# An edge-message kernel: rows gathered by GpSimd alone, where SyncE brought seven groups row by row

## The chip, the core and the metric

The kernel runs on one core of a Trainium2 chip. The metric is the device time in microseconds of one execution. A profile was taken of one execution, and all engine names below are those of the profile: PE is the matrix engine TensorE (PEld its weight loads), DVE is VectorE, ACT is ScalarE, POOL is GpSimd, SP is SyncE, which here only issues DMAs and loads registers.

## What is computed

One layer of a graph network on 12,500 nodes with 128 features and 400,000 edges, sorted by their target `dst`; `src` is random. Each edge has 32 attributes. Cut to what matters:

```
h   = relu(layernorm(x))
m   = relu(concat(h[src], h[dst], ea) @ w1 + b1) @ w2 + b2
agg = segment_sum(m, dst)
gi  = agg @ w_ih + b_ih ;  gh = h @ w_hh + b_hh
r, z = sigmoid of the first two thirds of gi + gh
n   = tanh(third of gi + r * third of gh)
out = x + (1 - z) * n + z * h
```

All is float32. `w1` has three blocks of rows: for `h[src]`, for `h[dst]` and for the attributes.

## The kernel before

**Prelude.** The nodes are normalised, transposed into `hT_all` (kept on chip), and multiplied by the first block of `w1`; the product `A = h @ w1a`, 12,500 rows of 512 bytes, is written to DRAM. In this way an edge's part from its source node is one row of `A`.

**Edge loop.** Edges go in tiles of 128; eight tiles are a double group (391 of them, the first with five tiles), and a double group is done as two units of four tiles (782 units `u`, `k, h = divmod(u, 2)`). For a double group the kernel needs eight tiles of rows of `A`, one for each edge: buffer `G`, 128 partitions by 8 by 128 floats. Then, for each unit:

- `pre` (L576): TensorE adds the target node's part and the attributes' part, from `L` (a one-hot matrix of targets in its upper half, made by VectorE at L479 out of `Ld`, and the attributes in its lower half) and `RW` (rows of the target nodes' window and of `w1`);
- `add` (L595): VectorE adds the PSUM result to `G`, in place;
- `relu` (L601): ScalarE writes the relu to `RB`. With the relu of the second unit the buffer `G` comes free;
- `seg` (L614): TensorE sums the rows by target with one-hot weights `OH`; `take` (L622, L623) copies the sums of a double group out of PSUM.

After every 14 double groups a generator `node` does the gates for a block of 512 nodes, one step a unit.

**How rows come.** `gather(k)` (L125) issues eight indirect DMAs on POOL, one for each tile of 128 rows, with the row numbers in `src_i`. `G` is a pool of `GBUFS` = 8 buffers, and `gathers(u)` asks for a double group when the taker of its buffer (`taker`, `ring`) is near its end in program order; at run time the gather waits for the relu that frees the buffer. The first `RAW` = 8 double groups are gathered before `A` is there: they fetch rows of `x` instead, and `raw_stats`, `raw_fin`, `raw_h`, `raw_turn` normalise, transpose and multiply them within the loop.

Seven double groups (`by_hand`: 70, 122, 174, 225, 277, 329, 381) are not gathered by POOL. For each, SyncE issues 1024 DMAs of one row of 512 bytes into a buffer of their own, `G_sp` (L753). `job_indices` loads the row numbers (L739), one VectorE instruction multiplies them by 512 (L849), SyncE loads 32 of them at a time into registers (L747), and each DMA takes its source address from a register. `run_jobs(u, phase)` spreads the issues evenly over the units between two such groups, four times a unit.

**Orders.** The schedule is written by hand (`manual_schedule`): each engine does its instructions in program order. SyncE's queue holds, besides the row DMAs, the loads that the loop lives on: `fetch_d` (L472, two broadcast loads of `Ld` for two double groups), `fetch` (L463, the load of `L`'s attributes for two double groups), the index tiles `src_i` and `dst_i`, and the node blocks' `xb` and `out`. POOL's queue holds the gathers alone, once the loop runs. `L` and `Ld` have three buffers each; `L` for double groups `k + 4` and `k + 5` is asked for at `k`.

Of the kernel before, what the change touches and what calls it, by code (L numbers as in the profile page):

```python
# [8 lines left out]
F32 = mybir.dt.float32  # L9
F16 = mybir.dt.float16  # L10
I32 = mybir.dt.int32
U8 = mybir.dt.uint8
BF16 = mybir.dt.bfloat16
ET = mybir.EngineType
AF = mybir.ActivationFunctionType
ALU = mybir.AluOpType
AX = mybir.AxisListType

N, E, D, DE = 12500, 400000, 128, 32
T = E // 128  # L20

GRP = 4
PAIR = 2 * GRP
SUP0 = T % PAIR
NP = T // PAIR + 1
# [11 lines left out]
NT = -(-N // 128)  # L37
NFULL = N // 128
BAT = (4,) + (8,) * 11 + (NFULL - 92, 1)
RAW = 8  # L40
GBUFS = 8
PLACE = 20
CH = PLACE * PAIR
LOAD = 32
STEP = 2
SP_PAIRS = 7
NR = 12672

ROW = 512


@with_exitstack
def tile_gnn(ctx: ExitStack, tc: tile.TileContext, x, src, srcT, dstT, dstP, eaT, eaP, w1, b1, w2T, b2,
             wih, bih, whh, bhh, out):
    nc = tc.nc
    ctx.enter_context(tc.manual_schedule())
    const = ctx.enter_context(tc.tile_pool(name="const", bufs=1))
    hT_all = const.tile([128, N], F32, name="hT_all")
    gp = ctx.enter_context(tc.tile_pool(name="gp", bufs=GBUFS))
    p2 = ctx.enter_context(tc.tile_pool(name="p2", bufs=2))  # L60
# [5 lines left out]
    def tiles(k):  # L66
        return (0 if k == 0 else SUP0 + (k - 1) * PAIR, SUP0 + k * PAIR)


    def unit_tiles(u):  # L70
        k, h = divmod(u, 2)
        t0, t1 = tiles(k)
        return [(t0 + a * GRP + j, j, a) for j in (2 * h, 2 * h + 1) for a in range(2)
                if t0 + a * GRP + j < t1]

    JOBS0 = 14

    by_hand = [JOBS0 + 5 + int((i + 1) * (NP - 15 - JOBS0) / SP_PAIRS) for i in range(SP_PAIRS)]


    src_i = {}
# [23 lines left out]
    A = dram.tile([N, D], F32, name="A")  # L105
# [2 lines left out]

    G = {}

    taker, ring = {}, []
    for k in range(NP):
        if k not in by_hand:
            taker[k] = ring[-GBUFS] if len(ring) >= GBUFS else -1
            ring.append(k)

    def gather(k):
        if k >= NP or k in by_hand:
            return
        G[k] = gp.tile([128, GRP, 2, D], F32, name="G")  # L120
        table = x if k < RAW else A
        for u in (2 * k, 2 * k + 1):
            for t, j, a in unit_tiles(u):
                c, i = divmod(t, CH)
                nc.gpsimd.indirect_dma_start(  # L125
                    out=G[k][:, j, a, :], out_offset=None, in_=table,
                    in_offset=bass.IndirectOffsetOnAxis(ap=src_i[c][:, i:i + 1], axis=0))

    for k in range(RAW):
        gather(k)  # L130
# [58 lines left out]
    with tc.tile_pool(name="pp", bufs=3) as pp:  # L189
# [50 lines left out]
        rows = const.tile([1, 6 * D + D], F32, name="rows")  # L240
# [18 lines left out]
        def chunk(q):  # L259
            b, c = chunks[q]  # L260
            i0, n = bats[b]
            return b, i0, c, min(n, c + 4), PB(b), (i0 + c) * 128
# [3 lines left out]
        for q in range(NC + 3):  # L266
            if q < NC:
                b, i0, c, e, P, n0 = chunk(q)
# [3 lines left out]
            if 1 <= q <= NC:  # L272
                b, i0, c, e, P, n0 = chunk(q - 1)
# [6 lines left out]
            if q >= 3:  # L280
                b, i0, c, e, P, n0 = chunk(q - 3)
# [4 lines left out]
            if q < NC:  # L286
                b, i0, c, e, P, n0 = chunk(q)
# [4 lines left out]
            if 1 <= q <= NC:  # L292
                b, i0, c, e, P, n0 = chunk(q - 1)
# [3 lines left out]
            if q >= 3:  # L297
                b, i0, c, e, P, n0 = chunk(q - 3)
                if e == bats[b][1]:
                    nc.sync.dma_start(nodes(A, i0, e, P), asb[b][:P, :e, :])  # L300
            if 2 <= q <= NC + 1:
                b, i0, c, e, P, n0 = chunk(q - 2)
# [4 lines left out]
        for b0, b1, n in ((0, 1, BAT[0]), (1, 12, 8), (12, 13, BAT[12])):  # L307
            i0 = sum(BAT[:b0])
            for b in range(b0, b1):
                i = i0 + (b - b0) * n  # L310
# [32 lines left out]
    for a in range(2):  # L343
        s = slice(V * a, V * (a + 1))
        nc.vector.tensor_scalar(node_of[s, :], base_b[s, :, a], place_c[s, :], float(-V * a),
                                op0=ALU.add, op1=ALU.add)
# [110 lines left out]
    def fetch(q):  # L457
        if q * QP >= NP:
            return
        n = min(QP, NP - q * QP)  # L460
        Ls[q] = p3.tile([128, QP * 512], F32, name="L")
        c = slice(q * QP * 512, (q * QP + n) * 512)
        nc.sync.dma_start(Ls[q][2 * V:, :n * 512], eaP[:, c])  # L463
# [72 lines left out]
    def slots(u):  # L536
        return [(j % 2) * 2 + a for _, j, a in unit_tiles(u)]

    def raw_h(u):
        if u < 2 * RAW:  # L540
            for i, s in enumerate(slots(u)):
                relu_norm(unit(u)[:, s, :], unit(u)[:, s, :], HE[u][:, i, :])

    def raw_stats(u):
        if u < 2 * RAW:
            l = slots(u)
            HE[u] = bn_sqrt(p2, bn(p2, lambda j: unit(u)[:, l[j], :], 128, len(l)), 128, len(l))

    def raw_fin(u):
        if u < 2 * RAW:  # L550
            n = len(slots(u))
            st = p2.tile([128, GRP, 2], F32, name="st_raw", bufs=4)
            bn_fin(p2, st[:, :n, :], HE[u], 128, n)
            HE[u] = st

    def raw_turn(u):
        if u < 2 * RAW:
            l = slots(u)
            pt = ps1.tile([128, 512], F32, name="misc")
            for i, s in enumerate(l):  # L560
                nc.tensor.transpose(pt[:, i * 128:(i + 1) * 128], unit(u)[:, s, :], ident)
            hT = p3.tile([128, 512], F32, name="hTe", bufs=2)
            nc.vector.tensor_copy(hT[:, :len(l) * 128], pt[:, :len(l) * 128])
            HE[u] = hT
# [163 lines left out]
        return o  # L728


    late = ExitStack()
    pj = late.enter_context(tc.tile_pool(name="pj", bufs=1, side="right"))
    NJ = len(by_hand)
    A_bytes = A.bitcast(U8).rearrange("n f -> (n f)")
    at = const.tile([NJ, PAIR * 128], I32, name="at")

    def job_indices(r):
        t0 = tiles(by_hand[r])[0]
        nc.sync.dma_start(at[r:r + 1, :], src[t0 * 128:(t0 + PAIR) * 128].rearrange(  # L739
            "(o e) -> o e", o=1))  # L740

    def one_by_one(r):
        k = by_hand[r]
        G[k] = pj.tile([128, GRP, 2, D], F32, name="G_sp")
        rows = G[k].bitcast(U8)
        for e0 in range(0, PAIR * 128, LOAD):
            _, vals = nc.values_load_multi_w_load_instructions(  # L747
                at[r:r + 1, e0:e0 + LOAD], engines=[ET.SP], min_val=0, max_val=ROW * (N - 1),
                skip_runtime_bounds_check_because="src holds numbers of nodes")
            for i, v in enumerate(vals):  # L750
                e = e0 + i
                a, j = divmod(e // 128, GRP)
                nc.sync.dma_start(rows[e % 128:e % 128 + 1, j, a, :],  # L753
                                  A_bytes[bass.ds(v, ROW)].rearrange("(o f) -> o f", o=1))
                if i % STEP == STEP - 1:
                    yield


    PH = 4
    live = []  # L760

    def run_jobs(u, phase):
        if phase == 0:
            for r, k in enumerate(by_hand):
                begin = 2 * by_hand[r - 1] + 2 if r else 2 * JOBS0
                if u == begin:
                    live[:] = [one_by_one(r), u, 2 * k - 8 - begin, 0]
        if live:
            it, begin, span, _ = live
            want = -(-(PAIR * 128 // STEP) * ((u - begin) * PH + phase + 1) // (span * PH))  # L770
            while live and live[3] < want:
                live[3] += 1
                if next(it, "end") == "end":
                    live.clear()


    asked = [RAW]

    def gathers(u):
        while asked[0] < NP and (asked[0] in by_hand or 2 * taker[asked[0]] + 1 < u + 2):  # L780
            gather(asked[0])
            asked[0] += 1

# [46 lines left out]
    for u in range(NU):  # L830
        k, h = divmod(u, 2)
        gathers(u)
        if h == 0:
            if k % QP == 0:
                fetch_d(k // QP + 3)
                fetch(k // QP + 2)
            if k % BP == 0 and k:
                nodes_left.append([node(k // BP - 1), 0])
            if k % PLACE == 1:
                indices(k // PLACE + 2)  # L840
            if k % PLACE == 5:
                place(k // PLACE + 1)
                dst_tile(k // PLACE + 2)
            if k == NP - 20:
                check_windows()
        for r in range(u, min(u + 1, NJ)):
            job_indices(r)
        if u == 2 * JOBS0 - 2:
            nc.vector.tensor_scalar(at, at, float(ROW), None, op0=ALU.mult)  # L849

        def other(phase):
            run_jobs(u, phase)
            if h == 0 and phase == 1:
                window(k + 3)
            if h == 0 and phase == 3:
                window_rows(k + 3)
            if phase == 3:
                step(nodes_left)

        other(0)  # L860
        if h == 0:
            take(k - 1)
        stages(u)
        other(1)
        other(2)
        seg(u)
        if u == 0:
            node_setup()
        other(3)
# [4 lines left out]

    late.close()
    fb = ctx.enter_context(tc.tile_pool(name="fb", bufs=1, side="right"))

    def general_setup():  # L880
# [94 lines left out]
    f = nc.values_load(flag[0:1, 0:1], min_val=0, max_val=1)  # L975
# [67 lines left out]
```

## Time and profile before

| what | value |
|---|---|
| time, median of 3 runs | 5573.1 us (5562.81, 5573.1, 5592.95) |
| profiled execution, its own time | 5562.81 us |
| span of the profiled execution | 5561.0 us |
| granted TensorE clock, mean | 0.674 |
| busy: PE, PEld | 2693.6 us (48%), 1588.2 us (29%) |
| busy: DVE, ACT, POOL | 1494.3 us (27%), 678.7 us (12%), 2932.6 us (53%) |
| indirect gathers of `A` on POOL (L125) | 3008, mean 955 ns |
| row DMAs on SP (L753) | 7168 of 0.5 KB |
| DMA engines' time taken by POOL's queue, SP's queue | 14.5%, 8.9% |

The busy shares are means over the whole span; no engine is near 100%. In the lists of waits, a line gives who waited, for whom, the time in total, the number of times and the longest; "remote" is a wait that the profile can't put down to an instruction. In a timeline, a line gives the start and the length in us, engine, source line, operation and tiles, how many instructions are merged, and in brackets the idle time ahead of them with what ended it. SP's instructions are only issues: the length is that of issuing, not of the transfer.

### The profile page before, as it was taken

What the parts mean: (1) busy time and instruction counts of PE and PEld (TensorE: products, weight loads), DVE (VectorE), ACT (ScalarE), POOL (GpSimd) and SP (SyncE); (2) the same over time, 40 slices, a digit from 0 to 9 for tenths busy, and PEclk for the clock granted to TensorE, in tenths of its full rate; (3) what the DMA queues carried; (4) which work ended last, traced back from release to release, by engine and by line L of the source; (5) the groups of instructions that cost most, each with busy time, mean ns of one, the idle gap of its engine ahead of it and who ended that gap; (6) DMA issues with size and microseconds to landing.
All of it is one profiled execution on the core that took longest, in us unless ns stands there. A gap on an engine that the chain in (4) does not pass through costs nothing. (4 is left out here: it accounts for less than half of the span.)

```text
span 5561.0 us, 57483 instructions
## 1 busy us (share of the span) xinstructions
PE 2693.6 (48%) x12938; PEld 1588.2 (29%) x12938; DVE 1494.3 (27%) x4097; ACT 678.7 (12%) x1460; POOL 2932.6 (53%) x3077
## 2 busy tenths in 40 slices
PE   4554554455445544444444454444455445544446
PEld 3432222232222322222222232222222222322223
DVE  5522222222222222222222222222222222222223
ACT  3211111111011111111111111100111111111111
POOL 4455555555455555455555546555455554655452
PEclk8766666676666666666666676666676666666667
DMA  3322222222122222222222222222222222222121
GB/s 118 72 62 58 65 60 58 74 57 63 51 63 54 68 58 57 55 63 67 57 55 61 60 66 57 58 59 58 71 58 57 61 55 56 68 62 59 51 63 52
DMA packets 168791, 342.80 MB, mean 62 GB/s; under 512 B 70653, under 2 KB 83752, under 8 KB 168447
## 3 DMA queue, kind: packets, MB, share of 16 engines
q0 software_dynamic: 98208, 201.33, 14.5%
q1 hardware_dynamic: 70095, 137.71, 8.9%
q8 instruction: 107, 1.75, 0.1%
q14 instruction: 237, 1.94, 0.1%
q10 hardware_dynamic: 144, 0.07, 0.0%
HBM read 324.99 MB, written 13.84 MB: 61 GB/s over the span
## 5 line engine op out<-in xcount | busy, mean ns | idle before, releaser
L125 POOL DMA_INDIRECT G<-A,src_i x3008 | 2873.8, 955 | 2550.7 <-ACT RB L601 1269.7
L576 PE MATMUL pre<-RW,L 128*128 128x256 f32 x3128 | 1231.4, 530 | 1820.1 <-DMA L<-in_eaP 1467.5
L576 PEld LDWEIGHTS pre<-RW,L 128*128 128x128 f32 x3128 | 740.6, 260 | 2178.7 <-issue 2025.8
L622 DVE COPY sums<-seg 64x128 f32<-64x128 f32 x391 | 110.1, 282 | 2602.9 <-PE seg L614 1183.5
L601 ACT ACTIVATE RB<-G 128x512 f32<-128x512 f32 x752 | 474.3, 631 | 1746.3 <-DVE G L595 844.7
L614 PE MATMUL seg<-RB,OH 128*32 128x129 f32 x6250 | 642.4, 340 | 3.5 <-issue 3.5
L501 PE MATMUL oh<-w1b,hw 128*64 128x128 f32 x782 | 204.4, 351 | 749.8 <-DVE hw L498 537.7
L595 DVE TENSOR_TENSOR G<-pre,G 128x512 f32<-128x512 f32 x752 | 514.1, 684 | 11.2 <-PE pre L576 0.3
L510 DVE TENSOR_TENSOR RW<-oh,b1b 32x128 f32<-32x128 f32 x782 | 219.6, 281 | 802.1 <-remote 284.1
L614 PEld LDWEIGHTS seg<-RB,OH 128*32 128x32 f32 x6250 | 348.9, 130 | 259.8 <-issue 167.7
L623 ACT CAST dcol<-seg 64x1 f16<-64x1 f32 x391 | 60.5, 155 | 2805.5 <-DVE sums L622 1873.3
L501 PEld LDWEIGHTS oh<-w1b,hw 128*64 128x64 f32 x782 | 88.4, 160 | 930.0 <-DVE hw L498 650.5
L479 DVE TENSOR_SCALAR L<-Ld,node_of 64x512 f32<-64x512 int32 x391 | 187.0, 478 | 0.2 <-issue 0.2
L528 DVE TENSOR_TENSOR OH<-dloc,iota 128x256 f32<-128x256 f16 (+1 forms) x392 | 165.9, 423 | 7.9 <-issue 0.6
L645 PE MATMUL nd<-spot,sums 64*128 64x40 f32 x782 | 131.4, 341 | 17.2 <-issue 17.2
L645 PEld LDWEIGHTS nd<-spot,sums 64*128 64x128 f32 x782 | 128.0, 254 | 30.6 <-issue 30.6
L630 DVE TENSOR_TENSOR TOT<-nd,TOT 128x192 f32<-128x192 f32 x28 | 10.0, 358 | 411.2 <-remote 344.2
L650 PE MATMUL misc<-spot_h,dcol 128*128 128x40 f16 x391 | 37.5, 200 | 153.2 <-issue 153.2
L609 PE MATMUL seg<-zrow 1*64 1x129 bf16 x391 | 102.7, 263 | 0.0
L498 DVE COPY hw<-hT_all 128x64 f32 x391 | 86.0, 220 | 17.4 <-DVE G L595 9.3
L305 PE MATMUL pre<-w1a,hT_all 128*128 128x128 f32 x196 | 51.6, 412 | 60.2 <-remote 30.2
L664 PE MATMUL misc<-DEG,brow 33*128 33x512 f32 x112 | 77.5, 778 | 0.1
(143 smaller groups left out, 1242.2 us busy)
## 6 DMA issues: line engine op xcount, KB each, us to landing
G_sp<-A SPq DMA_DIRECT2D x7168, 0.5 KB
Ld<-in_dstP SPq DMA_DIRECT2D x390, 128.0 KB
L<-in_eaP SPq DMA_DIRECT2D x195, 256.0 KB
G<-A,src_i POOLq DMA_INDIRECT x3008
xb<-in_x SPq DMA_DIRECT2D x28, 256.0 KB
out<-xb SPq DMA_DIRECT2D x28, 256.0 KB
xs<-in_x SPq DMA_DIRECT2D x11, 512.0 KB
A<-asb SPq DMA_DIRECT2D x11, 512.0 KB
```

Of the source, the lines that this page charges most:

```text
L125: nc.gpsimd.indirect_dma_start(out=G[k][:, j, a, :], out_offset=None, in_=table, in_offset=bass.IndirectOffsetOnAxis(ap=src_i[c][:, i:i + ...
L479: nc.vector.tensor_scalar(Ls[k // QP][:2 * V, c], Ds[k // QP][:, c], node_of[:, k:k + 1], None, op0=ALU.is_equal)
L501: nc.tensor.matmul(PB_[k][:2 * V, :D], hw.rearrange("p a v -> p (a v)"), w1b, start=True, stop=True)
L510: nc.vector.tensor_tensor(RW[k % 4][s, a, :], pm[s, :D], b1b[s, :], op=ALU.add)
L528: nc.vector.tensor_tensor(o, d.to_broadcast(shape), i.to_broadcast(shape), op=ALU.is_equal)
L576: nc.tensor.matmul(PP[u][:, 2 * i:2 * i + 2, :], Ls[k // QP][:, c0:c0 + 128], RW[k % 4], start=True, stop=not raw)
L595: nc.vector.tensor_tensor(RT[u], PP.pop(u), RT[u], op=ALU.add)
L601: nc.scalar.activation(o[:, :, :D], RT.pop(u), AF.Relu)
L609: nc.tensor.matmul(SEG[k][:2 * V, :D + 1], zrow[:, :2 * V], zrow[:, :D + 1], start=True, stop=False)
L614: nc.tensor.matmul(SEG[k][V * a:V * (a + 1), :D + 1], OH[k][:, j, a, :], RB[u % 3][:, (j % 2) * 2 + a, :D + 1], start=False, stop=all(b != ...
L622: nc.vector.tensor_copy(sums[:, k % BP, :], pm[:2 * V, :D])
L645: nc.tensor.matmul(pt[:, bass.ds(offs[i], V + SHIFT)], sums[:, i, :], spot, start=False, stop=i == n - 1)
```

## The change

The seven double groups are gathered by POOL like all others. `by_hand`, `taker`, `ring`, the pool `pj` with `G_sp`, the table `at`, `job_indices`, `one_by_one` and `run_jobs` are taken out with all that they issue. `RAW` and `GBUFS` become 9: the pool `G` has nine buffers, and nine double groups take rows of `x`. `gathers(u)` asks for double group `k` when group `k - 9` is near its end. The loop's other steps and their order stay.

```
-RAW = 8
-GBUFS = 8
+RAW = 9
+GBUFS = 9
-LOAD = 32
-STEP = 2
-SP_PAIRS = 7
-ROW = 512
...
-    JOBS0 = 14
-    by_hand = [JOBS0 + 5 + int((i + 1) * (NP - 15 - JOBS0) / SP_PAIRS) for i in range(SP_PAIRS)]
...
-    taker, ring = {}, []
-    for k in range(NP):
-        if k not in by_hand:
-            taker[k] = ring[-GBUFS] if len(ring) >= GBUFS else -1
-            ring.append(k)
     def gather(k):
-        if k >= NP or k in by_hand:
+        if k >= NP:
             return
...
-    def one_by_one(r):
-        k = by_hand[r]
-        G[k] = pj.tile([128, GRP, 2, D], F32, name="G_sp")
-        rows = G[k].bitcast(U8)
-        for e0 in range(0, PAIR * 128, LOAD):
-            _, vals = nc.values_load_multi_w_load_instructions(
-                at[r:r + 1, e0:e0 + LOAD], engines=[ET.SP], min_val=0, max_val=ROW * (N - 1),
-                skip_runtime_bounds_check_because="src holds numbers of nodes")
-            for i, v in enumerate(vals):
-                e = e0 + i
-                a, j = divmod(e // 128, GRP)
-                nc.sync.dma_start(rows[e % 128:e % 128 + 1, j, a, :],
-                                  A_bytes[bass.ds(v, ROW)].rearrange("(o f) -> o f", o=1))
-                if i % STEP == STEP - 1:
-                    yield
...
     def gathers(u):
-        while asked[0] < NP and (asked[0] in by_hand or 2 * taker[asked[0]] + 1 < u + 2):
+        while asked[0] < NP and 2 * (asked[0] - GBUFS) + 1 < u + 2:
             gather(asked[0])
             asked[0] += 1
...
-        for r in range(u, min(u + 1, NJ)):
-            job_indices(r)
-        if u == 2 * JOBS0 - 2:
-            nc.vector.tensor_scalar(at, at, float(ROW), None, op0=ALU.mult)
...
-            run_jobs(u, phase)
```

More of the change, by code (lines that the diff above doesn't have):

```diff
@@ L728, in gates @@
         return o
[L731 to L740, printed above, removed]
-    def one_by_one(r):
-        k = by_hand[r]
-        G[k] = pj.tile([128, GRP, 2, D], F32, name="G_sp")
-        rows = G[k].bitcast(U8)
-        for e0 in range(0, PAIR * 128, LOAD):
-            _, vals = nc.values_load_multi_w_load_instructions(
-                at[r:r + 1, e0:e0 + LOAD], engines=[ET.SP], min_val=0, max_val=ROW * (N - 1),
-                skip_runtime_bounds_check_because="src holds numbers of nodes")
-            for i, v in enumerate(vals):
-                e = e0 + i
-                a, j = divmod(e // 128, GRP)
-                nc.sync.dma_start(rows[e % 128:e % 128 + 1, j, a, :],
-                                  A_bytes[bass.ds(v, ROW)].rearrange("(o f) -> o f", o=1))
-                if i % STEP == STEP - 1:
-                    yield
[L759 to L774, printed above, removed]
     asked = [RAW]
     def gathers(u):
-        while asked[0] < NP and (asked[0] in by_hand or 2 * taker[asked[0]] + 1 < u + 2):
+        while asked[0] < NP and 2 * (asked[0] - GBUFS) + 1 < u + 2:
             gather(asked[0])
@@ L873, in tile_gnn @@
         run(it)
-    late.close()
     fb = ctx.enter_context(tc.tile_pool(name="fb", bufs=1, side="right"))
```

## The prediction

> **What bounds the kernel now.** I read the summary of waits first, then SyncE's own timeline, then POOL's, and went back to the prelude for what they left unexplained.
>
> ```profile
> PE pre L576 <- DMA L<-in_eaP: 1467.5, 118, 24.8
> POOL G L125 <- ACT RB L601: 1269.7, 153, 22.4
> ```
>
> Columns: who waited, for whom, us in total, times, longest. TensorE waits for `L`, the edge attributes, and POOL waits for a row buffer that ScalarE's relu must free. TensorE is 48% busy, POOL 53%: neither is full. Why is `L` late? SyncE's timeline over one period, and TensorE's at the same place:
>
> ```profile
> 826.76 23.03 SPq L753 DMA_DIRECT2D G_sp<-A  x36
> 849.89 0.79 SPq L472 DMA_DIRECT2D Ld<-in_dstP  x2
> 850.95 0.30 SPq L463 DMA_DIRECT2D L<-in_eaP  x1
> ```
>
> ```profile
> 854.85 2.04 PE L576 MATMUL pre<-RW,L 128*128 128x256 f32 x4 [9.52 <-DMA L<-in_eaP]
> ```
>
> 36 row transfers (L753) stand ahead of two `Ld` loads and one `L` load in SyncE's order; `L` is issued at 850.95, and 3.9 us later its first matmul starts, after 9.52 us of idle TensorE. The rows never let up: jobs of 1024 rows run from 343.2 to 1099.8, 1121.1 to 1843.7, and so on to 5472.8, 0.69 to 0.74 us a row. So SyncE is full from 343 to 5473 us, and the pace of the edge loop is its pace. Where `L` was issued 10 us or less before its matmul (129 pairs of groups after group 40), a double group takes 14.58 us by the relus.
>
> **But a second limit lies close behind.** One gather (L125) takes 0.95 us and the next starts 1.25 us after it, so eight make 10.0 us a double group; POOL does this in runs. Two places without any row transfer, group starts 279 to 341 and the prelude:
>
> ```profile
> 279.09 0.94 POOL L125 DMA_INDIRECT G<-A,src_i  x1 [5.21 <-ACT RB L601]
> ...
> 302.58 0.95 POOL L125 DMA_INDIRECT G<-A,src_i  x1 [3.50 <-ACT dcol L623]
> ...
> 341.47 0.94 POOL L125 DMA_INDIRECT G<-A,src_i  x1 [8.84 <-ACT RB L601]
> ```
>
> ```profile
> 313.07 0.69 DVE L595 TENSOR_TENSOR G<-pre,G 128x512 f32<-128x512 f32 x1
> 336.51 0.28 DVE L622 COPY sums<-seg 64x128 f32<-64x128 f32 x1 [22.75 <-remote]
> ```
>
> ```profile
> 57.96 0.18 DVE L162 BATCH_NORM_AGGREGATE mv<-bn 128x2 f32<-128x6 f32 x1 [1.22 <-DVE mv L162]
> 59.36 0.18 DVE L162 BATCH_NORM_AGGREGATE mv<-bn 128x2 f32<-128x6 f32 x1 [1.22 <-DVE mv L162]
> ...
> 88.76 0.51 DVE L162 BATCH_NORM_AGGREGATE mv<-bn 128x2 f32<-128x6 f32 x6 [1.21 <-DVE mv L162]
> ```
>
> POOL gathers without a pause from 302.58 to 332.6. In that run VectorE stands still from 313.8 to 336.5, waiting for matmuls that the trace has started at 312.7; 3.9 us after the run ends, it goes on. In the prelude POOL gathers from 3.2 to 79.4, and six aggregates that take 0.51 us together after it come 1.40 us apart within it. The rows tell the same: sorted by how long POOL had been gathering without a pause, the median from one row's issue to the next is 0.32 us in the first 2 us, about 0.7 from 4 to 12, 1.4 from 12 to 16, 2.1 from 16 to 20, and 0.32 again 2 us after the run. A long run of gathers makes everybody else's signals late; what carries them I can't see. POOL then runs out of free buffers, pauses, and the others catch up.
>
> **The change part by part.**
>
> *Row transfers, registers, tables taken out (L747, L753, L739, L849).* 7168 issues, 224 register loads, seven loads and one 0.67 us VectorE instruction go. What counts is the order of SyncE's queue: `Ld` and `L` loads then wait for buffers alone. Without rows, before 343 us, `L` was issued 35 to 68 us ahead of its first matmul, so the 1467.5 us wait goes. What is late next is not a load but POOL's buffer, by the cycle above.
>
> *Seven groups go to POOL.* 56 gathers, of which 8 are the new raw ones: 48 more of `A`, 48 x 1.25 = 60 us of POOL. Each waits for a relu that frees its buffer; behind it on POOL stand only later gathers, and the additions of its own group wait for it. In the sum they are groups at the loop's price like the others, and 1.25 us for 128 rows stands against 128 x 0.70 = 90 us on SyncE. The Trainium skill (Perfetto Trace Analysis, section DMA Optimizations) advises the opposite: where descriptor generation is the limit, spread DMAs over sync, scalar and GPSIMD. By that rule alone POOL's 60 us would be added and the time would be 5623 us; this trace shows SyncE, not POOL, without slack.
>
> *RAW 8 to 9.* Eight more gathers of `x` at the start: 10 us on POOL between 79.4 and 173.5, where it idles 93.94 us; without that cover they would cost those 10 us. The two additional raw units cost statistics, 8 transposes and 8 matmuls in the turnover of the raw groups, which runs at (279.09 - 173.50) / 8 = 13.2 us a group; I charge the ninth at that.
>
> *One pool of nine.* Eight plus the single `G_sp` were nine before, so it is the same memory. A deeper ring lets POOL run further ahead; where POOL waits for the relu, that moves when the wait falls, not how long. I put it at 0. Its ends: a run of three groups instead of two at the longest pause of 8.84 us is (30 + 8.84) / 3 = 12.9 us a group, at the shortest of 3.5 us 11.2; a run that starves the others more is rival 1.
>
> *Pace of the loop without rows.* No long stretch shows it, so I bound it. Row-free and released by a relu at both ends: group 16 starts on POOL at 279.09, group 21 at 341.47, 62.4 / 5 = 12.48 us a group. By relus of units 16 and 28: (344.26 - 275.50) / 6 = 11.46. With rows, but `L` not late, seven stretches of 6 to 26 groups: 11.66, 12.36, 12.59, 12.63, 12.95, 14.0, 14.46, mean 12.98; the part of the first that has rows (344.3 to 612.2) gives 13.4. From below: the shortest pause (3.5 us) after the longest run (30 us, three groups) gives 11.2. I take 12.48, the row-free one, as it has POOL's runs and pauses in it. It holds no node block, which is against it, and no SyncE competing, as after the change.
>
> **The sum**, on the profiled execution: it took 5562.81 us, 1.8 of it outside its span of 5561.0. It is the lowest of the three runs; their median, 5573.1, is 0.2% above it.
> - to the first gather of `A`: 173.5
> - nine groups at 13.2: 118.8
> - groups 18 to 390, 373 at 12.48: 4655.0
> - from POOL's last gather (5504.0) to the end (5561.0): 57.0, kept, because then as now about eight gathered groups and a node block follow
> - outside the span: 1.8
>
> Together 5006 us, 10% less. Fixed are 351.1 us, so each 0.1 us a group is 37 us, and the kernel before is met at (5562.8 - 351.1) / 373 = 13.97 us a group.
>
> **Rivals.**
> 1. *Slower: starvation takes the place of the late load.* Each wait for `L` now forces POOL to pause (it gathers 71% of the time from 350 to 5450) and the queue of signals to drain. Without it runs grow, and a group costs what the longest row-free pause says: a run of two groups and 8.84 us, 14.4 us a group; 351 + 373 x 14.4 = 5722 us. For it: two of the seven stretches, 14.0 and 14.46; VectorE's 22.75 us wait after 11 us of a run; the added node work. Against it: five stretches below 13, and 14.58 where `L` is late. It decides from 13.97 us a group.
> 2. *POOL becomes the bound.* If the starving came mostly from the rows, POOL would never pause: 351 + 373 x 10.0 = 4081 us. For it: TensorE's work, at 6.9 us a group (2693.6 / 391), and VectorE's, 3.8, fit into 10. Against it: both row-free places starve.
> 3. *The change doesn't free the loads.* SyncE's issues are themselves slow while POOL runs; if `L` stayed late for that alone, only POOL's 60 us would be felt, within some 1% of before. Against it: 35 to 68 us of lead before 343 us.
>
> **How the numbers follow.** About 0.5% is what can be told from no change. The forecast's case has 0.80: from 11.2 us a group (4529) to 13.7, midway between 13.4 and the first slow stretch, 14.0 (5461). Rival 1 has 0.12, rival 3 0.03, rival 2 0.05. The range 4510 to 5460 is the first case with its bounds. Faster by over 0.5%: 0.80 + 0.05 = 0.85; within: 0.03; slower: 0.12.
>
> **What would show it.** In the changed profile no L753; TensorE's wait for `L` near zero; `L` issued tens of us ahead; POOL's share at 10.0 / 12.48 = 80% of the loop counting its gaps, in runs of 16 to 24 gathers and pauses of 3 to 9 us released by the relu; VectorE's long waits for `seg` inside those runs. The step on the row-free pace is wrong if POOL runs without pauses, or if runs get longer than 24 and pauses longer than 9 us; the step on SyncE is wrong if TensorE still waits for `L`.

## The result, and the profile after

| | before | after |
|---|---|---|
| median of 4 runs each | 5575.1 us (5562.81 to 5592.95) | 5023.4 us (5009.07 to 5032.93) |
| ratio, 95% interval | | 0.9006 [0.8973, 0.9039] |
| profiled execution, its span | 5562.81, 5561.0 | 5009.07, 5006.8 |
| granted TensorE clock | 0.674 | 0.693 |

The forecast was 5006. The profile of the changed kernel, first its busy shares and the group of gathers (busy time, mean ns of one, idle time ahead of them):

```profile
PE 2635.2 (53%) x12962; PEld 1565.6 (31%) x12962; DVE 1499.5 (30%) x4124; ACT 678.2 (14%) x1470; POOL 2973.4 (59%) x3133
...
L111 POOL DMA_INDIRECT G<-A,src_i x3056 | 2907.2, 951 | 1945.1 <-issue 875.7
```

48 more gathers than before, and POOL idles 606 us less ahead of them (2550.7 in the kernel before). In the summary of waits no line has TensorE waiting for `L`; the wait for POOL's buffer has halved, from 1269.7 us, and the longest is VectorE's for the sums (who waits, for whom, us, times, longest):

```profile
DVE sums L608 <- remote: 1520.4, 139, 26.3
...
POOL G L111 <- ACT RB L587: 621.2, 125, 12.2
```

SyncE's timeline, two periods of loads:

```profile
1004.72 0.78 SPq L458 DMA_DIRECT2D Ld<-in_dstP  x2
1008.26 0.48 SPq L449 DMA_DIRECT2D L<-in_eaP  x1
1021.97 0.78 SPq L458 DMA_DIRECT2D Ld<-in_dstP  x2
1022.84 0.54 SPq L449 DMA_DIRECT2D L<-in_eaP  x1
```

Between these loads SyncE has little to do; its own longest wait is for a buffer of `Ld`, which VectorE must have read:

```profile
SPq L458 <- DVE L L465: 2198.0, 100, 36.5
```

`L` is issued 36 to 66 us ahead of its first matmul for nine pairs of groups in ten, and never less than 17.7, where the median before was 4.0. POOL's timeline, only the gathers that end a pause:

```profile
1014.99 0.94 POOL L111 DMA_INDIRECT G<-A,src_i  x1 [3.23 <-ACT dcol L609]
...
1038.68 0.94 POOL L111 DMA_INDIRECT G<-A,src_i  x1 [4.04 <-ACT dcol L609]
...
1062.11 0.94 POOL L111 DMA_INDIRECT G<-A,src_i  x1 [3.72 <-ACT RB L587]
```

So POOL gathers from 1014.99 to 1034.6 without a pause (1038.68 - 4.04). VectorE in that run:

```profile
1026.12 0.69 DVE L581 TENSOR_TENSOR G<-pre,G 128x512 f32<-128x512 f32 x1
1037.89 0.28 DVE L608 COPY sums<-seg 64x128 f32<-64x128 f32 x1 [11.08 <-remote]
```

It stands still for 11 us, 7.8 of them while POOL gathers, and goes on 3.3 us after the run has ended, as in the kernel before. Over the loop (groups 18 to 390, a pause being an idle time of over 0.5 us) the runs are of 8 (63 times), 16 (100), 24 (33) and 32 gathers (2). The 199 pauses are 4.8 us in the mean, against 7.4 before; 48 are under 3 us, 21 over 9, the longest 10.05.

### The profile page after: what moved, and what is told of

The parts are those of the page before. It is cut to its first block, busy times and chain, and to the rows that moved or that the text cites. A ratio compares the mean times of both kernels' runs of the same rounds, so it can differ in the third digit from the quotient of the medians.

```text
span 5006.8 us, 43030 instructions
## 1 busy us (share of the span) xinstructions
PE 2635.2 (53%) x12962; PEld 1565.6 (31%) x12962; DVE 1499.5 (30%) x4124; ACT 678.2 (14%) x1470; POOL 2973.4 (59%) x3133
## 4 chain that ended last, share of the span: by engine, by line
PE 36%; another core or an unknown queue 32%; issue 15%; DVE 12%; POOL 2%; ACTq 1%; DMA 1%; DVEq 1%; ACT 0%; SPq 0%; POOLq 0%
PE pre L562 13%; PE seg L600 9%; DVE G L581 4%; PE oh L487 3%; POOL G L111 2%; PE nd L631 2%; PE nd L650 1%; PE nd L654 1%; PE seg L595 1%; DVE OH L514 1%; ACTq L587 1%; DVE RW L496 1%; PE misc L650 1%; PE misc L652 1%
## 5 line engine op out<-in xcount | busy, mean ns | idle before, releaser
L111 POOL DMA_INDIRECT G<-A,src_i x3056 | 2907.2, 951 | 1945.1 <-issue 875.7
L562 PE MATMUL pre<-RW,L 128*128 128x256 f32 x3128 | 1148.3, 500 | 304.0 <-DVE G L581 148.3
L487 PE MATMUL oh<-w1b,hw 128*64 128x128 f32 x782 | 215.1, 367 | 1751.4 <-DVE hw L484 1271.6
L562 PEld LDWEIGHTS pre<-RW,L 128*128 128x128 f32 x3128 | 694.2, 243 | 629.1 <-issue 525.3
L608 DVE COPY sums<-seg 64x128 f32<-64x128 f32 x391 | 110.1, 281 | 2048.3 <-remote 1520.4
L631 PE MATMUL nd<-spot,sums 64*128 64x40 f32 x782 | 146.3, 347 | 115.0 <-issue 114.8
L631 PEld LDWEIGHTS nd<-spot,sums 64*128 64x128 f32 x782 | 145.0, 272 | 120.7 <-issue 120.7
L650 PE MATMUL nd<-DEG,brow 33*128 33x512 f32 x112 | 81.6, 816 | 1.0 <-DVE DEG L618 1.0
L654 PE MATMUL nd<-TOT,w2ih 128*128 128x512 f32 x112 | 79.0, 796 | 0.0
```

Source lines behind the costliest of these rows:

```text
L111: nc.gpsimd.indirect_dma_start(out=G[k][:, j, a, :], out_offset=None, in_=table, in_offset=bass.IndirectOffsetOnAxis(ap=src_i[c][:, i:i + ...
L487: nc.tensor.matmul(PB_[k][:2 * V, :D], hw.rearrange("p a v -> p (a v)"), w1b, start=True, stop=True)
L562: nc.tensor.matmul(PP[u][:, 2 * i:2 * i + 2, :], Ls[k // QP][:, c0:c0 + 128], RW[k % 4], start=True, stop=not raw)
L631: nc.tensor.matmul(pt[:, bass.ds(offs[i], V + SHIFT)], sums[:, i, :], spot, start=False, stop=i == n - 1)
L650: nc.tensor.matmul(pg, brow[:, c], DEG[:, :BW], start=True, stop=False)
```

## The experiments

**Two conditions.** The sessions on the chip were of two kinds, and no number below can be understood without this. In some, others' signals are late while POOL gathers, as in the profile that the prediction was made from; in others they are not. The kernel before takes 5549 to 5757 us in the one and 3957 to 3969 in the other. All kernels of one session were alike, and two chips showed both conditions in different sessions. "Late" and "prompt" are names for what the timelines show: instructions of other engines start long after what they wait for. Some of these gaps are put down to nothing that the profile shows ("issue"), so whether a signal or the instruction itself comes late isn't separated. VectorE's aggregates in the prelude, while POOL gathers, tell which it is; they write separate columns, so none needs the result of the one before. One and the same kernel (the changed one with eight buffers) in two sessions; first with late signals:

```profile
56.76 0.18 DVE L148 BATCH_NORM_AGGREGATE mv<-bn 128x2 f32<-128x6 f32 x1 [1.22 <-DVE mv L148]
58.16 0.18 DVE L148 BATCH_NORM_AGGREGATE mv<-bn 128x2 f32<-128x6 f32 x1 [1.22 <-issue]
59.56 0.18 DVE L148 BATCH_NORM_AGGREGATE mv<-bn 128x2 f32<-128x6 f32 x1 [1.22 <-DVE mv L148]
```

then with prompt ones:

```profile
45.62 0.62 DVE L148 BATCH_NORM_AGGREGATE mv<-bn 128x2 f32<-128x6 f32 x8
```

One aggregate every 1.40 us in the first, eight in 0.62 us in the second. The pair of the result, and the prediction's profile, are of the first kind. The experiments follow in the order of the question; each is told with its condition, and where expectations give numbers for one condition only, they were written before the other was known.

### Prompt signals: what the edit does there

`rows_out_8`, the changed kernel with eight buffers and eight raw groups:

```
-RAW = 9
-GBUFS = 9
+RAW = 8
+GBUFS = 8
```

> Row transfers out, but RAW and GBUFS stay 8. Theory A (SyncE's row issues made L late; without them the gather-and-pause cycle sets 12.46 us a double group): 5000 to 5060 us, within 1% of the changed kernel (5023). Rival B (the gain comes from the ninth buffer and the ninth raw group): within 1% of the kernel before, 5520 to 5620 us.

Measured, prompt: 4029.3 us (4019 to 4034) against 3962.1 (3957 to 3969) of the kernel before; ratio 1.0159 [1.0136, 1.0181]. Its gathers and the longest waits but one:

```profile
L111 POOL DMA_INDIRECT G<-A,src_i x3064 | 2950.4, 963 | 961.8 <-issue 909.6
```

```profile
DVE G L581 <- DMA G<-A,src_i: 1547.1, 600, 5.5
```

Nearly all of POOL's idle time is the 0.30 us between one gather and the next (3064 x 0.30 = 919 us); it never pauses in the loop, and VectorE waits for the rows themselves. Here POOL is the bound, as the prediction's second rival had it, at 10.1 us a double group, and seven groups given to it cost 67 us, 9.6 each. Taking rows off SyncE gains nothing, because nothing waited for it.

`three_rows` and, in another session, `three_rows_b`: the kernel before with three groups by rows instead of seven.

```
-SP_PAIRS = 7
+SP_PAIRS = 3
```

> The kernel before with 3 double groups brought singly in place of 7, pools of 8 as before. Theory A: 3072 rows at 0.70 us are 2150 us, SyncE has slack, L is issued over 20 us ahead, POOL has 380 of 391 double groups; 4930 to 5080 us. Rival B (buffers): 5520 to 5620 us. Rival C (each row also costs the others signals, so the loss grows with the number of rows and not at a threshold): 3/7 of the way from 5023 to 5575, 5200 to 5320 us.

> Three double groups singly, eight buffers, RAW 8. Where the kernel before takes about 5575: theory A, SyncE has slack, L is 20 us and more ahead, 12.45 us a double group on POOL: 4900 to 5080 us; rival B (the ninth buffer and ninth raw group make the gain): 5500 to 5620 us; rival C (loss in proportion to the rows): 5200 to 5320 us. Where it takes 3962: 3990 to 4010 us again.

Measured, both prompt: 3999.9 us (ratio 1.0098 [1.0077, 1.0119]), and 4004.1 beside 3964.0 of the kernel before, single runs. Four groups more on POOL cost 38 and 40 us, 9.5 to 10 each. SyncE's timeline:

```profile
1002.23 2.53 SPq L753 DMA_DIRECT2D G_sp<-A  x8
```

A row costs 0.32 us, less than half of the 0.70 that the prediction read. So with prompt signals the edit, group by group, makes the kernel slower; the changed kernel as it stands was not run in that condition.

### What stands behind POOL

`plain_loads`, the changed kernel with each later group's rows brought by two plain SyncE loads of 256 KB of contiguous rows. It leaves out the choice of the rows by `src`, and so computes another sum; it also moves the gathers ahead of the loop behind the first loads of `L`.

```
...
+            for a in range(2):
+                r = r0 + a * GRP * 128
+                nc.sync.dma_start(G[k][:, :, a, :], A[r:r + GRP * 128, :].rearrange(
+                    "(j p) f -> p j f", p=128))
+            return
```

> The rows of A come from SyncE in two plain loads of 256 KB for each double group; they are contiguous rows, so the choice of rows by src is left out, and all else is computed. POOL issues nothing in the loop. Theory A with starving by POOL's runs of gathers: the loop goes at its engines' own pace, 5.4 us a double group as in the last stretch of before or up to 7 with the node blocks: 2350 to 3000 us, and no waits of VectorE for seg over some 5 us. Rival D (12.46 us is the loop's own pace, from its chain of engines; POOL only follows): 4700 to 5050 us.

Measured, prompt: 2317.4 us, a little under the range that the theory gave. Its busy shares:

```profile
PE 2087.6 (90%) x12962; PEld 1293.5 (56%) x12962; DVE 1475.8 (64%) x4124; ACT 684.6 (30%) x1470; POOL 66.2 (3%) x77
```

Without gathers in the loop TensorE is 90% busy at a clock of 0.946, and a group takes 5.5 us. With prompt signals the time is thus set by how the rows come, not by the arithmetic. The kernel was not run in a late session, and the contiguous rows may themselves come more cheaply than scattered ones.

`paced` and `paced_b` (the same kernel in two sessions): a small memset on POOL behind each gather of the loop, so that gathers come 1.34 us apart instead of 1.25.

```
+                if k >= RAW:
+                    nc.gpsimd.memset(idle, 0.0)
```

> The changed kernel with a GpSimd memset of 128x128 floats after each gather in the loop (0.20 us in the profile's prelude), so that gathers start 1.45 to 1.6 us apart in place of 1.25. Theory A with starving that builds up in a run and needs a rate above what the signals' path bears: pauses vanish or shrink, 11.6 to 12.8 us a double group, 4680 to 5130 us. Rival E (each gather delays the others by a fixed amount, however far apart): the pauses stay, 5500 to 5900 us.

> The changed kernel with a GpSimd memset of 128x128 floats after each gather in the loop, which on the chip where the kernel before takes 3962 us put gathers 1.335 us apart in place of 1.25 and gave 4293 us. On a chip where it takes 5575: theory A with starving that needs a rate, pauses shrink and a double group costs 10.8 to 12.0 us, 4380 to 4830 us; theory E, a fixed delay for each gather, pauses as before and 12.5 to 13.2 us, 5010 to 5280 us. On a chip where it takes 3962: 4270 to 4310 us again.

Measured, single runs: `paced`, prompt, 4292.7 us and 10.83 us a group, which is 8 x 1.34 and 0.1: POOL-bound. The spacing is less than the 1.45 to 1.6 us that was expected. `paced_b`, late, 5022.2 us and 12.47 us a group, as without the memset. Its POOL timeline:

```profile
1009.37 0.95 POOL L112 DMA_INDIRECT G<-A,src_i  x1 [0.16 <-issue]
1010.32 0.22 POOL L116 MEMSET idle<- 128x128 f32 x1
1010.71 0.95 POOL L112 DMA_INDIRECT G<-A,src_i  x1 [0.17 <-issue]
1011.65 0.22 POOL L116 MEMSET idle<- 128x128 f32 x1
1015.33 0.95 POOL L112 DMA_INDIRECT G<-A,src_i  x1 [3.46 <-ACT dcol L612]
```

Spacing the gathers by 0.09 us did not relieve the others: there are 143 pauses instead of 199, of 4.4 us in the mean instead of 4.8, POOL's share of the loop, its gaps and memsets counted, rose from 80 to 86%, and the pace stayed. The theory that the pause is needed because gathers come too densely, at 1.25 us, is not supported by this. Theory E is met in the time, but not in its pauses, which it had as before.

A version with one longer memset (`paced_c`, 128x288) gave no result: its tile does not fit into the on-chip memory that the kernel leaves.

`paced_d`, a second memset behind each gather, to 1.50 us.

```
+                    nc.gpsimd.memset(idle, 0.0)
+                    nc.gpsimd.memset(idle[:, 0:32], 0.0)
```

> The changed kernel with two memsets (128x128 and 128x32) after each gather, for some 1.42 to 1.50 us from gather to gather. Where the kernel before takes about 5575: theory Q (what carries signals serves one gather in about 1.40 us; POOL asks every 1.25 or 1.34 us, so a queue grows and others stand in it; the total stays what that service allows, as 1.25 and 1.34 gave the same 12.45 us a double group): above 1.40 no queue grows, pauses vanish, 8 x 1.42 to 1.50 = 11.4 to 12.0 us a double group, 4590 to 4840 us. Theory H (12.45 us a double group for another reason, POOL's pace is only swallowed by the pauses): 5000 to 5040 us. Where the kernel before takes 3962: POOL alone, 8 times its interval, 4520 to 4820 us.

Measured, prompt by its own prelude (eight aggregates in 0.62 us), a single run: 4986.2 us, 12.67 us a group. That misses the range for prompt signals: 8 x 1.50 is 12.0, and a pause of some 0.7 us a group stands behind most groups, in which POOL waits for nothing that the profile shows. As the signals were prompt, the run doesn't tell the two theories on late signals apart; that stays open.

### Late signals: where the gain comes from

`after_again` and `after_third`, the changed kernel as it stands, in two sessions more.

> The changed kernel again, because the runs of the kernel before beside the first experiments took 3962 us where it had taken 5575. If signals are on time here too (the kernel before near 3962), theory F holds: POOL's back-to-back gathers set the time, the change adds 48 of them at 1.25 us, 60 us, and it takes 4010 to 4030 us, 1.2 to 1.7% slower than before. If signals are late in POOL's runs (the kernel before near 5575), theory A: 5000 to 5040 us. Rival G, that the changed kernel is the faster one in either condition: under 3940 us beside 3962.

> The changed kernel as it stands. If signals are late while POOL gathers: 4976 to 5040 us, as twice before. If they are prompt: POOL gathers without a pause, 10.0 us a group, and the ninth buffer is worth nothing: within 15 us of the version with eight buffers, 4015 to 4045 us, 1.3 to 2.1% above the kernel before; a rival in which the ninth buffer lets POOL start the loop earlier gives under 4010.

Measured, both late: 4996.1 us (ratio 0.8978 [0.892, 0.9036]) and 5062.0 (0.8859 [0.8814, 0.8905]); the first is 4 us below its range, the second 22 us above, beside a kernel before of 5703.9. The gain of 10 to 11% was there in all three sessions with late signals in which the changed kernel ran as it stands. The loop took 12.43 and 12.69 us a group.

`rows_out_8_b`, eight buffers again, in the session of `after_third`.

> The changed kernel with eight buffers and eight raw groups. If signals are late while POOL gathers: theory A (the ninth buffer only lengthens POOL's runs and its pauses alike, and the pace is that of the others' late work): within 40 us of the changed kernel beside it, with runs of 8 and 16 gathers and no run of 24. Rival C (a run that fills more buffers spreads one pause over more groups): 0.4 to 0.8 us a group more, 5170 to 5330 us. If signals are prompt: 4029 us, between 4015 and 4045.

Measured, late: 5042.1 us, 0.8844 [0.8809, 0.888] of the kernel before; to `after_third` it is 0.995 [0.986, 1.003], worked out from the single times. The ninth buffer is worth nothing that can be measured. One detail was wrong: 18 runs have 24 gathers, although only 16 fit into two free buffers; some buffer comes free while a run lasts.

`eleven_rows`, the kernel before with eleven groups by rows.

```
-SP_PAIRS = 7
+SP_PAIRS = 11
```

> The kernel before with 11 double groups brought singly in place of 7. On a chip where the kernel before takes 3962 us, theory F (POOL's gathers back to back set the time, SyncE has slack at 0.32 us a row): 4 groups less on POOL at 10.0 us, 3915 to 3930 us; rival: SyncE full already, over 3970. On a chip where it takes 5575, theory A (SyncE's rows, slowed by POOL's runs, set the time): 11264 rows at 0.5 to 0.7 us from 343 us on, 6000 to 8300 us; rival B (rows are not what sets the time): under 5600.

Measured, late: 7191.5 us beside 5757.2, single runs. The wait that answers to the 1467.5 us:

```profile
PE pre L576 <- DMA L<-in_eaP: 3665.8, 148, 35.8
```

Rows go without end from 326 to 7100 us, 0.60 us each, POOL gathers in 53% of the loop, and a group takes 18.9 us (7100 less 326 us are 11264 x 0.60). SyncE's row issues set the pace here.

`five_rows`, with five.

```
-SP_PAIRS = 7
+SP_PAIRS = 5
```

> The kernel before with five groups brought row by row instead of seven. If signals are late while POOL gathers: theory A (SyncE's queue sets the pace only where its rows don't fit beside the loop; 5 x 1024 rows x 0.70 us = 3584 us fit into some 4800 us): L is no longer waited for, POOL's cycle of 12.46 us a group holds for the other groups, 5023 less 5 x 12.46 = 4961 us, between 4880 and 5080, below both kernels or level with the changed one. Rival B (each row costs the loop something, fitting or not, in proportion: 5023 + 5/7 x 552): 5417 us, above 5200. If signals are prompt: POOL's gathers set the time, two more groups at 10 us than the kernel before: 3982 us, between 3970 and 3995; by a rival in which rows cost the loop something there too, below 3962.

Measured, late: 5282.3 us (5223 to 5311), ratio 0.9274 [0.923, 0.9319]. It is by the bound given (5200) on the rival's side, and 135 us under the rival's price. The theory's range, 4880 to 5080, is missed. The summary of waits of its profiled execution (its fastest, 5222.8 us):

```profile
PE pre L576 <- DMA L<-in_eaP: 50.1, 8, 9.1
```

and SyncE's timeline:

```profile
2018.64 23.49 SPq L753 DMA_DIRECT2D G_sp<-A  x30
2042.23 0.79 SPq L472 DMA_DIRECT2D Ld<-in_dstP  x2
2043.11 0.48 SPq L463 DMA_DIRECT2D L<-in_eaP  x1
```

`L` is seldom waited for, with a lead of 37 us in the median, and yet the kernel is 220 us slower in the median than the one without rows beside it (1.041 [1.028, 1.053] of it by the means; 208 us without the slowest of its four runs). The wait for `L` is 50 us of this in the profiled execution. So five groups of rows cost 44 us each (220 / 5), net of POOL's work for them.

That SyncE had slack, as theory A had it, does not follow from the lead alone. SyncE's own wait for a free buffer, the counterpart of the 2198.0 us in the changed kernel, is

```profile
SPq L472 <- DVE L L479: 178.0, 26, 32.1
```

and its five jobs of rows run from 342 to 5092 us, 0.87 to 0.95 us a row where the theory took 0.70. The queue was all but full with five groups too. How much of the 220 us is the queue's, and how much is what rows do to the other engines, no run separates; `three_rows` with late signals might, but both its runs fell in prompt sessions.

Of the 642 us between seven groups and none, measured on these two kernels and the one before beside them, 422 come with the first two taken out and 220 with the other five. If those two cost 44 us each like the others, 334 us were the late load's; that split is worked out, not measured. In POOL's timeline the cost shows as longer pauses: 5.7 us in the mean and POOL's share 76%, against 5.2 and 79% in `after_third` (the fastest of four runs here, the slowest there).

## Why the prediction was right, and where it was not

**The pace without rows, 12.48 us a group: right.** Measured 12.456 over groups 18 to 390, and 12.43, 12.69 and (eight buffers) 12.54 in other executions. The stretch of five groups that it was read from was typical; that it came within 0.03 us of it is in part luck, since the other readings that the prediction lists go from 11.2 to 14.46, and the changed kernel's own executions differ by 0.26. (The seven stretches with rows have a mean of 12.95 as listed, not 12.98; nothing was worked out from it.)

**The sum, term by term, in the profiled execution:**

| term | predicted | measured |
|---|---|---|
| to the first gather of `A` | 173.5 | 182.2 |
| nine groups | 118.8 | 116.2 |
| groups 18 to 390 | 4655.0 | 4643.3 |
| last gather to the end | 57.0 | 65.1 |
| outside the span | 1.8 | 2.3 |
| sum | 5006 | 5009.1 |

That the sum is only 3 us off is luck: the terms are off by 8.7, -2.6, -11.7, 8.1 and 0.5 us, and these cancel. The medians, 5023 and 4996 to 5062 us in the three sessions, are the fairer measure.

**The cover for the ninth raw group: wrong, by 8.7 us.** The step cost its eight gathers of `x` at nothing, since POOL idles behind them. But POOL's idle time was not what mattered: while they last, VectorE's statistics, on which `A` depends, stay late. The aggregates of `after_third` (nine raw groups),

```profile
91.75 0.18 DVE L148 BATCH_NORM_AGGREGATE mv<-bn 128x2 f32<-128x6 f32 x1 [1.91 <-issue]
93.85 0.18 DVE L148 BATCH_NORM_AGGREGATE mv<-bn 128x2 f32<-128x6 f32 x1 [1.92 <-remote]
```

and of `rows_out_8_b` (eight) in the same session:

```profile
88.96 0.51 DVE L148 BATCH_NORM_AGGREGATE mv<-bn 128x2 f32<-128x6 f32 x6 [0.52 <-DVE mv L148]
```

With eight the backlog is worked off at 89 us; with nine it lasts past 97. The first gather of `A` is at 174.2 and 182.3. The prediction had seen the 1.40 us and priced them nowhere; without the cover it would have charged 10 us.

**SyncE full, and the load late for it: right at seven groups, but a row has no fixed price.** `eleven_rows` confirms that SyncE can set the pace, and without rows the wait for `L` is gone. `five_rows` shows that rows cost the loop something where the load is seldom late. The 0.70 us a row belong to the kernel that they were read in: with late signals rows came 0.60 us apart where POOL gathers in 53% of the loop (`eleven_rows`), and 0.87 to 0.95 where it does in 76% (`five_rows`). The sum didn't depend on this, since its pace came from a stretch with no rows at all; a prediction for five groups made from the same step would have been some 300 us too low (4961 against 5282).

**The pool of nine worth nothing: right** (0.995 [0.986, 1.003]).

**What would show it: seen in the main.** TensorE's wait for `L` is gone, POOL's share is 80.7% (80% predicted), and 1294 of the 1532 us of VectorE's waits over 5 us for `seg` (L608) fall into POOL's runs. The sizes are only partly as named: of the runs 63 are of 8 gathers and two of 32, of the pauses 48 are under 3 us and 21 over 9, and a third of them (72) are ended by the copy of the sums (`dcol`), not by the relu. By the prediction's own sign, runs over 24 with pauses over 9 us, its step on the pace would be in doubt; the measured pace says that these stayed too few to matter.

**The first rival, starvation in place of the late load at 14.4 us a group: did not come.** Runs of 24 gathers came 33 times where the kernel before had one, but the pauses shrank from 7.4 to 4.8 us in the mean.

**What it took for granted.** The prediction took the late signals for a property of the kernel. They are one of the session: with prompt ones the same kernels take 3962 to 4029 us, the second rival's mechanism rules (its price was 4081), and the sign turns round with eight buffers, since the kernel before then loses nothing to its rows. Forecast and result come from sessions of the same kind; that the result was not taken in a prompt one, where the version with eight buffers took 4029 us and was the slower one, was not secured by anything in the prediction. The rule weighed there, to spread DMAs over sync, scalar and GPSIMD where descriptor generation is the limit (the Trainium skill, Perfetto Trace Analysis, section DMA Optimizations), agrees with the prompt sessions, where seven groups on SyncE save 67 us, and not with the late ones, where they cost 550 to 640. No version that gathers the right rows was the fastest in both conditions.

**Open.** What carries the late signals, and why some sessions have them. That a gather holds some shared service for about 1.40 us, in which others' signals queue, would fit the 1.40 us between aggregates; by itself it makes 8 x 1.40 = 11.2 us a group, not the 12.45 that neither the spacing of gathers nor the buffers moved. No run here settles it.

## What to carry to other kernels

Before an engine's queue is called the bound, look whether its instructions cost the same throughout: a row DMA here took 0.32 us or, in the mean of a job, 0.6 to 0.95, by what POOL was doing and by the session. Look in a profile for a row of like instructions on one engine that is far slower beside another engine's run than after it (1.40 us against 0.08 an aggregate); where there is one, take the pace from a stretch that has the effect in it, price every instruction added to that run at what it delays, not at its engine's idle time, and measure a change in more than one session before its sign is believed.

## What had not been expected of the hardware

- One kernel, 3957 to 3969 us in one session and 5549 to 5757 in others, on the same kind of chip, and both on one and the same chip; the late signals go with it. The granted clock of this kernel does too (0.72 to 0.73 against 0.67 to 0.68), but it doesn't tell the condition: `paced_d`, prompt, has 0.673, and the changed kernel, late, 0.691.
- With late signals, gathers spaced from 1.25 to 1.34 us left the loop at 12.47 us a group; with prompt ones the loop took 10.83 with the same edit, against 10.1 without it (and with eight buffers).
- With late signals five groups of row DMAs cost the loop 44 us per 1024, although the load that they share a queue with was seldom waited for; rows came 0.60, 0.70 and 0.89 us apart where POOL gathered in 53, 70 and 76% of the loop (eleven, seven and five groups).
- With plain loads in place of the indirect gathers the loop runs at 5.5 us a group, and the granted clock is 0.946 instead of 0.73 (both with prompt signals).
